# Two attentions in one kernel: x^T of the second batch loaded a stage sooner, first scores in turns with queries, turned P written ahead of x, x in whole rows at the start

## The chip, the cores and the metric

The kernel runs on one core of one Trainium2 chip. A core has engines that run beside each other, each with its own list of instructions in a fixed order: PE (TensorE, the matrix products), DVE (VectorE), ACT (ScalarE), POOL (GpSimd) and SP (SyncE, which here issues nearly all DMAs). An instruction waits by semaphore for what it needs, and everything behind it on its engine waits too. The metric is the device time of a run in microseconds. Three runs of the kernel before took 825.4, 826.2 and 827.56 us; their median is 826.2 us.

## The reference

x is (2, 2048, 640), two batches of 2048 rows; the context is (2, 128, 384), of which the last 4 tokens are the adapter's. There are 8 heads of 80 columns; all is float32.

```python
enc, ca = ctx[:, :124], ctx[:, 124:]
query = x @ Wq
hs = mha(query, enc @ Wk, enc @ Wv)              # text attention, 124 keys
ca_q1 = einsum('btc,th->bch', ca, Wq_ca)          # (2, 384, 640)
ca_q1 = ca_q1[:, linspace(0, 383, 2048).astype(int), :]
ca_hs1 = mha(ca_q1, x, x)                         # keys and values are x itself
ca_hs2 = mha(ca_hs1 @ Wq, ca @ Wk_ca, ca @ Wv_ca) # 4 keys
out = (hs + ca_hs2) @ Wout + b_out + x
```

mha is softmax(q k^T / sqrt(80)) v by heads. The second attention has only 384 different query rows in a batch, so the kernel computes those and gathers its rows by index at the end.

## The kernel before, in words

**Blocks.** x is worked on in 8 blocks of 512 rows, (b, sb) with b the batch and sb from 0 to 3, and in 16 row tiles of 128 a batch. Products with Wq need x transposed. Block (0, 0) is loaded plainly into a buffer "xz" and transposed on PE (pt_x, `x_first`). Every other block comes by `x_block`: 8 DMAs (xi) gather pieces of 128 bytes into the same buffer "xz", of which there is one, and five DVE transposes of 32x32 squares (xt) finish the job. The transposed blocks lie in five slots (`Slots`); a block's slot is given back when its users are done. `slots.free(n)` is a condition on them. In the second batch each block is loaded twice: once for yz, once more ("again") for its queries.

**Adapter attention** for a batch: `yz_block` (pyz, pt_y) maps a block to its logits' factors, `maxima` makes scores s and reduces their maxima on DVE (mx), `less_maxima` folds the maxima in, and `contraction` makes the scores again, takes exp on ACT (ea) and accumulates against y (acc). Scores s go through one PSUM buffer of four banks, so an s waits for the engine that reads the one before.

**Text attention**: `queries` makes q of a block (pq, 5 column chunks c, each summed over 5 row chunks i of x^T), `scores` takes a unit m of two row tiles (sc, then maximum m and subtraction on DVE, exp on ACT, sum r on DVE, product on POOL), `turned` transposes P on DVE (eb), writes it to HBM (kept) and reads it back by keys (pT), `values` multiplies with the values and Wout (ph, po) and adds into the residual rows xo, which `residual` has loaded. `completed` adds gathered rows of the adapter to tiles that were stored early (xe, early).

**Order.** PE's instructions and SP's DMAs stay in the order in which the program writes them. That order is made by a small planner: a `Fill` is a list of stages that yield after pieces of PE work, `Mix` runs the fill that has had the least PE time (by its own costs), and `weave` runs a main line (the setup, maxima, contraction) and fills each gap, given in us, with pieces. `own` holds adapter blocks, `text` the queries and units, `again` the second loads. `together` steps several generators in turns, `chain` one after the other. `ahead(m)` is what is done for unit m: the residual and the turned P of unit m + 1, scores of unit m + 2, queries, and the values of m. A scheduler orders the other engines' instructions by their readiness. Pools set how much can be open: PSUM tiles of `mm_tile` come three at a time from ps_m, "xrow" holds four row tiles x, P turned (eb) and pT have one buffer each.

**The lines that the steps touch.** L345 to 365 load x, Wq and the first weights; L633 `x_first`; L647 `x_block`; L836 `queries`; L896 `turned`, L912 `residual`, L1034 `ahead`; from L1061 the plan.

Of the kernel before, what the change touches and what calls it, by code (L numbers as in the profile page):

```python
# [13 lines left out]
P = 128  # L14
# [135 lines left out]
def kernel(  # L150
# [194 lines left out]
    def load_grouped(dst, w):  # L345
        dma(dst[:, :4, :], w.rearrange("(c r) n -> r c n", c=4)[:P])
        for g in range(4):
            dma(dst[R * g : R * (g + 1), 4, :], w[D2 * g + P : D2 * (g + 1), :])

# [7 lines left out]
    for st in range(4):  # L357
        most, rest = by_chunk(x[0, st * P : (st + 1) * P, :])
        t = rows_of[:, st]
        dma(t[:, : 4 * P].rearrange("p (c d) -> p c d", c=4), most)  # L360
        dma(t[:, 4 * P :].rearrange("p (g d) -> p g d", g=4), rest)
        if st == 2:
            load_grouped(wq_sb, Wq)
# [269 lines left out]
    def x_first():  # L633

        t = x_tile(0, 0, False)
        flat = t.rearrange("p k c s -> p (k c s)")
        for n in range(4 * NCH):
            k, c = divmod(n, NCH)
            if n % 4 == 0:
                pt = mm_tile(f"pt_x_{n // 4}")  # L640
            transpose(
                pt[:, n % 4 * P : (n % 4 + 1) * P], rows_of[:, k, c * P : (c + 1) * P], ident
            )
            if n % 4 == 3:
                evacuate(flat[:, (n - 3) * P : (n + 1) * P], pt)
# [190 lines left out]
    def queries(n, chunks):  # L836

        t = xt["q", *blocks[n]]
        if n not in q_of:
            yield from room(n)  # L840
        for c in chunks:
# [192 lines left out]
    def ahead(m):  # L1034
# [4 lines left out]
        if m + 1 < units:  # L1039
            more = [residual(m + 1), turned(m + 1)]  # L1040
# [38 lines left out]
    Mix(pe, (text, 1)).run(5.0)  # L1079
# [3 lines left out]
    for sb in range(NSB):  # L1083
# [5 lines left out]
    text.add(  # L1089
        stage(("s", 0), scores(0)), stage("turned", together(turned(0), residual(0))),  # L1090
        stage(("s", 1), scores(1)),
        *[ahead(m) for m in range(units)],
    )
    weave(less_maxima(0, mx_of[0]), fill)
    ps_turns[:] = [ps_m]
    on[0] = "D"
    own.add(adapter_stages("x", 1, 0, slots.free(1), ("q", *blocks[NSB - 1])))
# [6 lines left out]
    own.add(adapter_stages("yz", 1, 0))  # L1104
    for sb in range(1, NSB):
        own.add(
            adapter_stages("x", 1, sb, slots.free(1)),
            adapter_stages("yz", 1, sb, ("half", 1, sb - 1)),
        )
# [3 lines left out]
            stage(("again", 1, sb), x_block(1, sb, True), slots.free(2), ("t", 2 * sb + 2))  # L1113
# [48 lines left out]
```

## Time and profile before

| | before |
|---|---|
| median of 3 runs | 826.2 us (825.4 to 827.56) |
| the profiled execution | 825.36 us, span 823.7 us |
| PE busy | 754.6 us (92%) |
| DVE, ACT, POOL busy | 379.4 (46%), 191.1 (23%), 134.5 (16%) us |
| mean granted TensorE clock | 0.969 |
| chain that ended last | PE 78%, DVE 8%, DMA 6%, SPq 2%, issue 2%, ACT 2%, POOL 1% |
| DMA moved | 96.94 MB in 151029 packets, 120197 of them under 512 B |

The span runs from the first to the last instruction of the profiled execution; its device time is 1.66 us longer. PE is the engine that is busy nearly all the time, and the chain of work that ended last goes through it for 78% of the span. The mean granted clock is a share of the full 2.4 GHz; in single stretches it is 1.0 or falls to 0.5. "SPq" and "PEq" are the sequencers of an engine, which issue DMAs or wait. The matmul's own line is L28, a helper's, so rows are told apart by the names of their tiles.

### The profile page before, as it was taken

Reading aid. Unit: us, or ns where it says so; the run is one execution under the profiler, and the core shown is the slowest. Engines: PE = TensorE matmul, PEld = TensorE weight load, DVE = VectorE, ACT = ScalarE, POOL = GpSimd, SP = SyncE. Lnnn points to the kernel's source line nnn. Section 1 sums busy time; section 2 is a strip of 40 time slices with the busy share of each in tenths; the row PEclk is TensorE's granted clock in tenths of the full one; section 3 lists DMA queues with packets and bytes.
Section 4 is the critical chain, followed back from the end, with each engine's and each line's share of the span. In section 5 each row is a group of like instructions: output and inputs, shape, how many; then the busy total and the mean of one; then the engine's idle time right before and its main releaser. Section 6 shows DMA issues by size and latency. Waiting matters only on the chain.

```text
span 823.7 us, 9364 instructions
## 1 busy us (share of the span) xinstructions
PE 754.6 (92%) x3785; PEld 386.3 (47%) x3785; DVE 379.4 (46%) x507; ACT 191.1 (23%) x232; POOL 134.5 (16%) x192
## 2 busy tenths in 40 slices
PE   4999999999779999981999997999999999999987
PEld 3663343333434445550444453543443456556654
DVE  1124655442743426563574956452230375255621
ACT  2021221113434344100212020044443421011100
POOL 6000000000111003220050503010010012542320
PEclk9999999999979999995999998999999999999999
DMA  9708414000152415676797984081320545977771
GB/s 250 171 1 134 63 13 64 1 0 1 52 167 68 128 40 153 192 133 96 186 207 165 214 204 84 21 187 38 99 52 17 85 146 156 249 203 191 211 205 63
DMA packets 151029, 96.94 MB, mean 118 GB/s; under 512 B 120197, under 2 KB 122565, under 8 KB 148938
## 3 DMA queue, kind: packets, MB, share of 16 engines
q1 hardware_dynamic: 145866, 85.75, 41.1%
q0 software_dynamic: 5120, 10.59, 8.0%
q8 instruction: 30, 0.49, 0.3%
q14 instruction: 13, 0.11, 0.0%
HBM read 64.14 MB, written 32.18 MB: 117 GB/s over the span
## 4 chain that ended last, share of the span: by engine, by line
PE 78%; DVE 8%; DMA 6%; SPq 2%; issue 2%; ACT 2%; POOL 1%; DVEq 0%; ACTq 0%; POOLq 0%
PE pq L28 21%; PE po L28 19%; PE s L28 11%; PE sc L28 8%; PE acc L28 5%; PE ph L28 5%; PE pyz L28 3%; SPq L222 2%; DMA pT<-kept 2%; DMA kept<-eb 2%; DVE xt L660 2%; DVE mx L711 2%; POOL p L892 1%; DVE p L880 1%; DMA xz<-in_x_dram 1%
## 5 line engine op out<-in xcount | busy, mean ns | idle before, releaser
L28 PE MATMUL po<-wout_sb,hsT 128*128 128x320 f32 x640 | 187.0, 440 | 0.0
L28 PE MATMUL pq<-xt,wq_sb 128*128 128x512 f32 x320 | 155.0, 621 | 7.0 <-DVE xt L660 5.8
L28 PEld LDWEIGHTS po<-wout_sb,hsT 128*128 128x128 f32 x640 | 119.7, 191 | 68.9 <-issue 24.8
L711 DVE TENSOR_REDUCE mx<-s 128x4 f32<-128x2048 f32 x48 | 109.5, 2281 | 84.8 <-PE s L28 84.8
L892 POOL TENSOR_TENSOR p<-p,r 128x992 f32<-128x992 f32 x32 | 61.3, 1915 | 438.5 <-DVE r L891 378.9
L761 ACT ACTIVATE ea<-s 128x1536 f32<-128x1536 f32 x64 | 92.6, 1447 | 107.0 <-PE s L28 107.0
L28 PEld LDWEIGHTS pq<-xt,wq_sb 128*128 128x128 f32 x320 | 59.6, 197 | 84.7 <-issue 72.4
L28 PE MATMUL sc<-kpad,q 128*128 128x248 f32 x384 | 96.8, 390 | 1.6 <-DVE r L775 1.6
L961 DVE TENSOR_TENSOR xo<-xo,po 128x320 f32<-128x320 f32 x64 | 30.4, 479 | 121.2 <-PE po L28 121.2
L28 PEld LDWEIGHTS sc<-kpad,q 128*128 128x128 f32 x384 | 69.7, 192 | 34.6 <-issue 22.1
L28 PE MATMUL s<-ca,yz 32*128 32x384 f32 x512 | 60.9, 545 | 6.2 <-ACT ea L761 6.0
L879 DVE TENSOR_REDUCE m<-sc 128x4 f32<-128x496 f32 x64 | 42.5, 664 | 42.7 <-PE sc L28 42.5
L28 PE MATMUL ph<-pT,vpad 128*32 128x256 f32 (+1 forms) x512 | 53.6, 399 | 9.0 <-DMA pT<-kept 8.6
L28 PE MATMUL s<-yz,ca 32*128 32x512 f32 x384 | 54.8, 640 | 5.7 <-DVE mx L711 5.5
L243 ACT COPY q<-pq 128x512 f32<-128x512 f32 x31 | 18.1, 585 | 172.1 <-PE pq L28 172.1
L901 DVE STREAM_TRANSPOSE eb<-p 128x1024 f32<-128x1024 f32 x32 | 39.1, 1234 | 40.8 <-POOL p L892 37.2
L28 PE MATMUL acc<-ea,y_sb 128*32 128x384 f32 x512 | 55.9, 509 | 0.0
L887 ACT ACTIVATE p<-p 128x992 f32<-128x992 f32 x32 | 33.0, 1030 | 96.4 <-DVE p L880 96.4
L973 POOL DMA_INDIRECT xo<-o,query x23 | 36.0, 1565 | 78.0 <-DVE m L879 29.9
L890 DVE TENSOR_REDUCE r<-p 128x8 f32<-128x992 f32 x32 | 37.8, 1181 | 19.4 <-ACT p L887 19.4
L880 DVE TENSOR_TENSOR p<-sc,m 128x496 f32<-128x496 f32 x64 | 42.9, 670 | 1.8
L28 PE MATMUL pyz<-xt,wyz 128*64 128x512 f32 (+1 forms) x96 | 25.3, 648 | 19.5 <-DVE xt L660 19.5
(137 smaller groups left out, 433.8 us busy)
## 6 DMA issues: line engine op xcount, KB each, us to landing
kept<-eb SPq DMA_DIRECT2D x16, 1024.0 KB, 5.7
pT<-kept SPq DMA_DIRECT2D x64, 256.0 KB, 5.4
xi<-in_x_dram SPq DMA_DIRECT2D x44, 256.0 KB, 4.8
xo<-in_x_dram SPq DMA_DIRECT2D x32, 320.0 KB, 3.5
out_dram<-xo SPq DMA_DIRECT2D x23, 320.0 KB, 2.3
early<-xo SPq DMA_DIRECT2D x9, 320.0 KB, 2.4
xe<-early SPq DMA_DIRECT2D x9, 320.0 KB, 7.0
out_dram<-xe SPq DMA_DIRECT2D x9, 320.0 KB, 3.2
```

The lines of the kernel that those rows point to most:

```text
L28: ins = self.tc.nc.tensor.matmul(out, lhsT, rhs, **kw)
L243: nc.scalar.copy(dst, src)
L711: nc.vector.tensor_reduce(mx[:, ct, u, :, sb], q4, AX.X, ALU.max)
L761: nc.scalar.activation(e, q4[:, :, :CAD], AF.Exp, scale=SCALE)
L879: nc.vector.tensor_reduce(m, s4, AX.X, ALU.max)
L880: nc.vector.tensor_tensor(e[:, 4 * u : 4 * u + 4, :NK], s4, m.unsqueeze(2).to_broadcast([P, 4, NK]), ALU.subtract,)
L887: nc.scalar.activation(et, et, AF.Exp, scale=SCALE)
L890: nc.vector.tensor_reduce(r, et, AX.X, ALU.add)
L892: nc.gpsimd.tensor_tensor(et, et, r.unsqueeze(2).to_broadcast([P, HEADS, NK]), ALU.mult)
L901: nc.vector.transpose(eb[:, :, k], e_of.pop(at).rearrange("p h (j b) -> p j h b", j=4))
L961: nc.vector.tensor_tensor(xr[k][:, cols], xr[k][:, cols], po[:, :HALF], ALU.add)
L973: nc.gpsimd.indirect_dma_start(out=t, out_offset=None, in_=o2_of[b], in_offset=bass.IndirectOffsetOnAxis(ap=query[:, st : st + 1], axis=0) ...
```

## The change

**Start.** The first block of x is loaded in four DMAs of whole rows (128x640) ahead of Wq, and four DVE copies collect each tile's last columns into x_last; before, each tile came in two DMAs, the last tile behind Wq. Wq comes in four DMAs of one chunk each and four small ones; before, the four chunks were one DMA. The first three column chunks of block 0's queries are now summed in turns over the row chunks i, in three PSUM tiles, and the share of text work ahead of the setup is 12.5 us of planned PE time instead of 5.0.

**First scores.** The scores of units 0 and 1 and the turned P of unit 0 run in turns with the query stages that are left, where they stood behind all of them.

**Turned P ahead of x.** In `ahead`, the turned P of the next unit (eb, kept) is written before its residual rows xo are loaded.

**Second batch.** Blocks 0 and 1 of the second batch are both loaded during the first contraction (block 1 was loaded at the start of the second maxima). The "again" loads for the queries may start with one free slot instead of two, and one unit sooner.

```diff
--- before.py
+++ after.py
@@ -342,11 +342,6 @@
 
     load_ca(0)
 
-    def load_grouped(dst, w):
-        dma(dst[:, :4, :], w.rearrange("(c r) n -> r c n", c=4)[:P])
-        for g in range(4):
-            dma(dst[R * g : R * (g + 1), 4, :], w[D2 * g + P : D2 * (g + 1), :])
-
     w_c = {}
 
     def load_w(name, w):
@@ -354,13 +349,12 @@
         dma(w_c[name], w.rearrange("(c p) n -> p c n", p=P))
 
     rows_of = block_rows("xz").rearrange("p (k n) -> p k n", k=4)
-    for st in range(4):
-        most, rest = by_chunk(x[0, st * P : (st + 1) * P, :])
-        t = rows_of[:, st]
-        dma(t[:, : 4 * P].rearrange("p (c d) -> p c d", c=4), most)
-        dma(t[:, 4 * P :].rearrange("p (g d) -> p g d", g=4), rest)
-        if st == 2:
-            load_grouped(wq_sb, Wq)
+    for k in range(4):
+        dma(rows_of[:, k], x[0, k * P : (k + 1) * P, :])
+    for c in range(4):
+        dma(wq_sb[:, c, :], Wq[D2 * c : D2 * c + P, :])
+    for g in range(4):
+        dma(wq_sb[R * g : R * (g + 1), 4, :], Wq[D2 * g + P : D2 * (g + 1), :])
     load_w("kca", Wk_ca)
     load_w("k", Wk)
 
@@ -634,13 +628,18 @@
 
         t = x_tile(0, 0, False)
         flat = t.rearrange("p k c s -> p (k c s)")
+        last = xrow.tile([P, H], F32, tag="x", name="x_last")[:, : 4 * P]
+        last = last.rearrange("p (k s) -> p k s", k=4)
+        for k in range(4):
+            nc.vector.tensor_copy(
+                last[:, k, :].rearrange("p (g d) -> p g d", g=4), by_chunk(rows_of[:, k, :])[1]
+            )
         for n in range(4 * NCH):
             k, c = divmod(n, NCH)
             if n % 4 == 0:
                 pt = mm_tile(f"pt_x_{n // 4}")
-            transpose(
-                pt[:, n % 4 * P : (n % 4 + 1) * P], rows_of[:, k, c * P : (c + 1) * P], ident
-            )
+            src = rows_of[:, k, D2 * c : D2 * c + P] if c < 4 else last[:, k, :]
+            transpose(pt[:, n % 4 * P : (n % 4 + 1) * P], src, ident)
             if n % 4 == 3:
                 evacuate(flat[:, (n - 3) * P : (n + 1) * P], pt)
 
@@ -838,6 +837,19 @@
         t = xt["q", *blocks[n]]
         if n not in q_of:
             yield from room(n)
+        if n == 0:
+
+            first, chunks = chunks[:3], chunks[3:]
+            pq = [mm_tile(f"pq_{n}_{c}") for c in first]
+            for i in range(NCH):
+                for c in first:
+                    matmul(
+                        pq[c], wq_of(i, c), t[:, :, i, :], start=(i == 0), stop=(i == NCH - 1)
+                    )
+                yield WITHIN
+            for c in first:
+                evacuate(q_of[n][:, c, :], pq[c])
+            yield
         for c in chunks:
             pq = mm_tile(f"pq_{n}_{c}")
             for i in range(NCH):
@@ -1037,7 +1049,7 @@
 
         parts, needs, more = [], [], []
         if m + 1 < units:
-            more = [residual(m + 1), turned(m + 1)]
+            more = [turned(m + 1), residual(m + 1)]
         more.append(completed())
         if m + 2 < units:
             parts.append(stage(("s", m + 2), scores(m + 2)))
@@ -1076,7 +1088,7 @@
         adapter_stages("yz", 0, 3, ("half", 0, 2)),
     )
     text = Fill(done, *[early(n) for n in range(NSB)])
-    Mix(pe, (text, 1)).run(5.0)
+    Mix(pe, (text, 1)).run(12.5)
     fill = Mix(pe, (own, 1), (text, 1))
     weave(setup_a2(), fill)
     own.parts.insert(0, adapter_stages("yz", 0, 0))
@@ -1086,23 +1098,22 @@
     fill.until(done, "values")
     sp_stack.close()
     open_late()
-    text.add(
-        stage(("s", 0), scores(0)), stage("turned", together(turned(0), residual(0))),
-        stage(("s", 1), scores(1)),
-        *[ahead(m) for m in range(units)],
+    first = chain(
+        stage(("s", 0), scores(0)), together(turned(0), residual(0)), stage(("s", 1), scores(1))
     )
+    text.parts[:] = [together(first, *text.parts), *[ahead(m) for m in range(units)]]
     weave(less_maxima(0, mx_of[0]), fill)
     ps_turns[:] = [ps_m]
     on[0] = "D"
-    own.add(adapter_stages("x", 1, 0, slots.free(1), ("q", *blocks[NSB - 1])))
+    own.add(adapter_stages("x", 1, 0, slots.free(1)), adapter_stages("x", 1, 1, slots.free(1)))
     weave(contraction(0, sq, 2.0), fill)
 
 
     begin(1)
     on[0] = "A"
     ps_turns[:] = [ps_m, ps_m, ps_m, ps_a]
-    own.add(adapter_stages("yz", 1, 0))
-    for sb in range(1, NSB):
+    own.add(adapter_stages("yz", 1, 0), adapter_stages("yz", 1, 1, ("half", 1, 0)))
+    for sb in range(2, NSB):
         own.add(
             adapter_stages("x", 1, sb, slots.free(1)),
             adapter_stages("yz", 1, sb, ("half", 1, sb - 1)),
@@ -1110,7 +1121,7 @@
     again = Fill(
         done,
         *[
-            stage(("again", 1, sb), x_block(1, sb, True), slots.free(2), ("t", 2 * sb + 2))
+            stage(("again", 1, sb), x_block(1, sb, True), slots.free(1), ("t", 2 * sb + 1))
             for sb in range(NSB)
         ],
     )
```

The order of the setup on PE: the last key product pk, the pa products of the adapter's key, and the first queries of block 1 (pq from xt_1; xt_0 is block 0). Before:

```order
32 L28 MATMUL pk_372<-ctxT,k_279 128x256 x3
33 L41 MATMUL pt_wq_0_381<-ident,wq_sb 128x128 x4
34 L41 MATMUL pt_wq_4_387<-ident,wq_104 128x128
35 L28 MATMUL pq_3_429<-xt_0_196,wq_sb 128x512
36 L28 MATMUL pa_301<-blk_kca,wqT_380 128x48 x5
37 L28 MATMUL pq_3_429<-xt_0_196,wq_sb 128x512 x2
38 L41 MATMUL pt_wq_0_439<-ident,wq_sb 128x128 x4
39 L41 MATMUL pt_wq_4_445<-ident,wq_104 128x128
40 L28 MATMUL pq_3_429<-xt_0_196,wq_sb 128x512 x2
41 L28 MATMUL pa_301<-blk_kca,wqT_438 128x48 x5
42 L28 MATMUL pq_4_456<-xt_0_196,wq_104 128x512 x5
43 L28 MATMUL pyz_0_0_472<-xt_0_196,wyz 64x512 x2
```

Here the queries of block 0 (pq_3, pq_4) stand between the last pk and pyz. After the change, with the same names:

```order
54 L28 MATMUL pk_400<-ctxT,k_292 128x256 x3
55 L28 MATMUL pa_317<-blk_kca,wqT_390 128x48 x5
56 L28 MATMUL pq_0_453<-xt_1_275,wq_sb 128x512 x2
57 L41 MATMUL pt_wq_0_457<-ident,wq_sb 128x128 x4
58 L41 MATMUL pt_wq_4_463<-ident,wq_104 128x128
59 L28 MATMUL pq_0_453<-xt_1_275,wq_sb 128x512 x2
60 L28 MATMUL pa_317<-blk_kca,wqT_456 128x48 x5
61 L28 MATMUL pq_0_453<-xt_1_275,wq_sb 128x512
62 L28 MATMUL pyz_0_0_484<-xt_0_195,wyz 64x512 x2
```

The first query product of block 1 moved to a place directly behind the last pk and one group of pa, and the pyz of block 0 now has one query product in front of it instead of five.

DVE, in the same place of the program after the change (kpad is made from pk, wyz from pa, xt_1 is the transposed block 1 for that query):

```order
26 L508 TENSOR_SCALAR kpad<-pk_357,side 128x2x124 x2
27 L508 TENSOR_SCALAR kpad<-pk_400,quarter 128x2x124 x4
28 L659 STREAM_TRANSPOSE xt_1_275<-xi_1_276 128x512 x4
29 L662 STREAM_TRANSPOSE xt_1_275<-xi_1_276 128x4x128
30 L399 TENSOR_SCALAR wyz<-pa_317,side 128x4x24
31 L402 TENSOR_SCALAR wyz_107<-pa_317,halves 128x24
32 L399 TENSOR_SCALAR wyz<-pa_317,side 128x4x24
33 L402 TENSOR_SCALAR wyz_107<-pa_317,halves 128x24
```

The transposes of block 1 moved from behind the wyz operations to the place between kpad and wyz.

The second maxima, SP's list. Before, xi_0, xi_1 and xi_2 are the loads for yz of the second batch, and kept, pT, xo belong to text units:

```order
87 L222 DMA xi_0_1917<-in_x_dram 32x16x32
88 L222 DMA pT_1952<-kept_1833 32x4x512 x4
89 L222 DMA xi_1_1971<-in_x_dram 32x64x32
90 L222 DMA xi_1_1971<-in_x_dram 32x16x32
91 L222 DMA xi_1_1971<-in_x_dram 32x64x32
92 L222 DMA xi_1_1971<-in_x_dram 32x16x32
93 L222 DMA xi_1_1971<-in_x_dram 32x64x32
94 L222 DMA xi_1_1971<-in_x_dram 32x16x32
95 L222 DMA xi_1_1971<-in_x_dram 32x64x32
96 L222 DMA xi_1_1971<-in_x_dram 32x16x32
97 L222 DMA out_dram<-xo_6_1631 128x640
98 L222 DMA xi_2_2063<-in_x_dram 32x64x32
```

The loads of blocks 1 and 2 for yz stand one behind the other, with one store between. After the change, xi_0 and xi_1 here are the second loads for queries, and xi_2 is block 2 for yz, some rows later in the list:

```order
99 L222 DMA xi_1_2032<-in_x_dram 32x16x32
100 L222 DMA kept_2049<-eb_2046 128x2048
101 L222 DMA xo_10_2051<-in_x_dram 128x640
102 L222 DMA xo_11_2053<-in_x_dram 128x640
103 L222 DMA xe_0_2055<-early_0_1366 128x640
104 L222 DMA xe_0_2055<-early_1_1414 128x640
105 L222 DMA xe_2_2058<-early_2_1577 128x640
106 L222 DMA xe_2_2058<-early_3_1626 128x640
107 L222 DMA xi_2_2126<-in_x_dram 32x64x32
108 L222 DMA xi_2_2126<-in_x_dram 32x16x32
```

The load of block 1 for yz has moved forward into the first contraction, and the second loads of blocks 0 and 1 have taken the places ahead of block 2.

DVE around those loads, after the change (mx are maxima of the adapter's scores, xo_9 a residual tile, eb the turned P, xt the transposed blocks):

```order
229 L973 TENSOR_TENSOR xo_8_1835<-xo_8_1835,po_8_1_2216 128x320
230 L710 TENSOR_REDUCE mx_1924<-s_1_1_0_1_2225 128x4
231 L710 TENSOR_REDUCE mx_1924<-s_1_1_1_0_2242 128x4
232 L973 TENSOR_TENSOR xo_9_1837<-xo_9_1837,po_9_0_2238 128x320
233 L659 STREAM_TRANSPOSE xt_1_2031<-xi_1_2032 128x512 x4
234 L662 STREAM_TRANSPOSE xt_1_2031<-xi_1_2032 128x4x128
235 L710 TENSOR_REDUCE mx_1924<-s_1_1_1_1_2260 128x4
236 L913 STREAM_TRANSPOSE eb_2321<-p_12_2062 128x4x256
237 L913 STREAM_TRANSPOSE eb_2321<-p_13_2153 128x4x256
238 L659 STREAM_TRANSPOSE xt_2_2125<-xi_2_2126 128x512 x4
239 L662 STREAM_TRANSPOSE xt_2_2125<-xi_2_2126 128x4x128
240 L710 TENSOR_REDUCE mx_1924<-s_1_1_2_0_2291 128x4
```

The transposes that empty the buffer of xi_1 stand behind xo_9_0, and those of xi_2 behind one mx and two eb. PE beside it:

```order
385 L28 MATMUL po_9_0_2238<-wout_sb,hsT_0_2075 128x320 x2
386 L28 MATMUL po_9_0_2238<-wout_sb,hsT_2_2145 128x320
387 L28 MATMUL s_1_1_1_0_2242<-yz_1_2096,ca_129 128x512 x4
388 L28 MATMUL po_9_0_2238<-wout_sb,hsT_2_2145 128x320
389 L28 MATMUL po_9_0_2238<-wout_sb,hsT_4_2170 128x320
390 L28 MATMUL pq_2_2255<-xt_0_1972,wq_sb 128x512 x4
391 L28 MATMUL s_1_1_1_1_2260<-yz_1_2096,ca_129 128x512 x4
392 L28 MATMUL pq_2_2255<-xt_0_1972,wq_sb 128x512
393 L28 MATMUL pyz_2_0_2269<-xt_2_2125,wyz 64x512 x2
394 L28 MATMUL pyz_2_1_2270<-xt_2_2125,wyz 64x512 x2
395 L28 MATMUL pyz_2_0_2269<-xt_2_2125,wyz_107 128x512
396 L28 MATMUL pyz_2_1_2270<-xt_2_2125,wyz_107 128x512
```

pyz of block 2 stands one query chunk and one s behind the last po_9_0.

The last unit, SP's list, before:

```order
214 L222 DMA out_dram<-xo_10_3814 128x640
215 L222 DMA out_dram<-xo_11_3816 128x640
216 L222 DMA xo_14_4040<-in_x_dram 128x640
217 L222 DMA xo_15_4042<-in_x_dram 128x640
218 L222 DMA kept_4047<-eb_4044 128x2048
219 L222 DMA pT_4076<-kept_4047 32x4x512 x4
```

The store of kept stands behind two stores and two loads. After the change:

```order
207 L222 DMA out_dram<-xo_10_3823 128x640
208 L222 DMA out_dram<-xo_11_3825 128x640
209 L222 DMA kept_4047<-eb_4044 128x2048
210 L222 DMA xo_14_4049<-in_x_dram 128x640
211 L222 DMA xo_15_4051<-in_x_dram 128x640
212 L222 DMA pT_4080<-kept_4047 32x4x512 x4
```

The store of kept moved ahead of the two loads of xo.

## Rows read from the trace of the kernel before

**Rows 1.** Page, totals: the span, and PE's busy time, share and instructions.
```profile
span 823.7 us, 9364 instructions
PE 754.6 (92%) x3785; PEld 386.3 (47%) x3785; DVE 379.4 (46%) x507; ACT 191.1 (23%) x232; POOL 134.5 (16%) x192
```

**Rows 2.** Waits of PE: us in total, times, longest.
```profile
PE pyz L28 <- DVE xt L660: 19.5, 1, 19.5
PE ph L28 <- DMA pT<-kept: 8.6, 2, 4.4
PE pt_x L41 <- DMA xz<-in_x_dram: 7.9, 2, 7.7
PE s L28 <- ACT ea L761: 6.0, 3, 4.4
PE pq L28 <- DVE xt L660: 5.8, 1, 5.8
PE s L28 <- DVE mx L711: 5.5, 3, 2.9
```

**Rows 3.** Stretch by PE, PEld, DVE, ACT, POOL busy; granted clock, DMA share, GB/s.
```profile
380.00:390.00 10.00, 0.00 (x0) 0.00 (x0) 0.19 (x1) 0.00 (x0) 0.00 (x0) 0.50 1.01 158
```

**Rows 4.** Timeline, start: start us, us long, engine, operation, [idle before <- releaser].
```profile
5.86 3.66 SPq L222 DMA_DIRECT2D wq_sb<-in_L_xattn_Wq_dram  x5
...
19.08 7.40 PE L28 MATMUL pq<-xt,wq_sb 128*128 128x512 f32 x12
26.32 0.84 PE L28 MATMUL p_kca<-caT,w_kca 128*128 128x8 f32 x7
```

**Rows 5.** Timeline of PE, 176 to 211, at the full clock.
```profile
176.58 5.42 PE L28 MATMUL pq<-xt,wq_sb 128*128 128x512 f32 x12
...
206.49 0.93 PE L28 MATMUL s<-ca,yz 32*128 32x384 f32 x8
207.35 0.85 PE L28 MATMUL acc<-ea,y_sb 128*32 128x384 f32 x8
208.13 2.78 PE L28 MATMUL sc<-kpad,q 128*128 128x248 f32 x12
```

**Rows 6.** DMA issues, 4 to 20: KB each, median us to landing.
```profile
wq_sb<-in_L_xattn_Wq_dram SPq DMA_DIRECT2D x1, 1280.0 KB, 10.0
...
xz<-in_x_dram SPq DMA_DIRECT2D x3, 64.0 KB, 8.0
```

**Rows 7.** Timeline, setup: PE's pa, DVE's kpad.
```profile
38.32 1.21 PE L28 MATMUL pa<-blk_kca,wqT 128*128 128x48 f32 x10
...
51.92 1.63 DVE L514 TENSOR_SCALAR kpad<-pk,quarter 128x248 f32<-128x248 f32 x4 [0.44 <-PE pk L28]
```

**Rows 8.** Timeline, first unit: ACT's exp, SP's store of kept, PE's first ph.
```profile
216.16 1.03 ACT L887 ACTIVATE p<-p 128x992 f32<-128x992 f32 x1 [2.71 <-DVE p L880]
...
222.54 0.36 SPq L222 DMA_DIRECT2D kept<-eb  x1
...
236.10 1.98 PE L28 MATMUL ph<-pT,vpad 128*64 128x256 f32 x8 [4.36 <-DMA pT<-kept]
```

**Rows 9.** Timeline, second batch: transposes, the next load, the pyz behind it.
```profile
375.13 2.48 DVE L660 STREAM_TRANSPOSE xt<-xi 128x512 f32<-128x512 f32 x4
...
378.23 9.10 SPq L222 DMA_DIRECT2D xi<-in_x_dram  x8
...
392.36 1.97 PE L28 MATMUL pyz<-xt,wyz 128*64 128x512 f32 x4 [19.50 <-DVE xt L660]
```

**Rows 10.** Timeline of SP: an x load while POOL issues gathers.
```profile
423.24 16.64 SPq L222 DMA_DIRECT2D xi<-in_x_dram  x8
```

**Rows 11.** Timeline, the last unit: SP's xo loads and kept, PE's last first ph.
```profile
787.30 2.20 SPq L222 DMA_DIRECT2D xo<-in_x_dram  x2
...
789.55 0.42 SPq L222 DMA_DIRECT2D kept<-eb  x1
...
804.39 4.58 PE L28 MATMUL ph<-pT,vpad 128*64 128x256 f32 x32 [4.25 <-DMA pT<-kept]
```

## The prediction

> **What bounds the kernel now.** I read the page's totals first: TensorE (PE) is busy 754.6 us, 92% of the span [rows 1]. Of what is left, almost all stands in one view, the waits of PE by what it waited for [rows 2]: 19.5 us once for the transposes of x (xt) ahead of pyz, 8.6 in two waits for the turned P (pT), 7.9 at the start for x, 6.0 for an exp, 5.8 for another xt, 5.5 for maxima. So a change gains only by shortening those waits, or by keeping the granted clock up: while PE stood still before the second batch, 0.50 was granted [rows 3], the 1.2 GHz level, and work behind a long wait starts at that level. Twelve pq matmuls took 7.40 us right after the first wait [rows 4] and 5.42 elsewhere [rows 5], so that dip cost 2.0; I price every dip behind a wait of over 4 us like it. The work of PE itself is the same before and after, so I go by stalls alone, place by place, against the profiled run of 825.36 us (span 823.7 and 1.66 around it); the median of the runs shown, 826.2, lies 0.84 above it.
>
> **1. Start: x in whole rows, Wq by chunks, three query chunks in turn.** In before the fourth tile of x is issued behind Wq, and PE waits for it; the queries start at 19.08 and p_kca, which needs its own weights, at 26.32 [rows 4]. In after all of x is issued ahead of Wq. The first Wq load went out at 5.86 [rows 4], where after's first will, and the load of 1280 KB needed 10.0 us to land [rows 6]. I take x complete at about 9, the last transposes and copies until about 12, and then queries paced by PE, with Wq's chunks landing one by one until 16 or 17: 15 chunk products (30 matmuls) at 5.42/12 x 2 = 0.9 us are 13.5, with 2.0 for the clock this gives 27.5 for p_kca. That is 1.2 later than before, but 9 products more are done, 9 x 0.9 = 8.1. Gain 6.9, I take 7. Bounds: 8.5 if p_kca comes at 26, 0 if x and Wq still land only at 18 together.
> Here the trace shows one Wq issue of 1280 KB that landed in 10.0 us with other loads in flight [rows 6]; no row of it shows Wq in smaller pieces. The Trainium skill ("DMA: Bandwidth & Descriptors", section "Measured (HBM→SBUF, 128 partitions, SWDGE, issued from GpSimd)") asks for loads batched to 1 MiB and more and calls transfers under 64 KB dominated by descriptors; by it the four pieces of 320 KB are a step back, and the sum would be that of rival (c) below.
>
> **2. The setup behind it: a new stall.** Because the queries of block 0 are done sooner, PE reaches the first query of block 1 before the vector engine (DVE) has its x^T. On DVE four kpad operations, 1.63 us [rows 7], and four transposes of x, 2.48 [rows 9], stand between the last pk and that query, 4.1 us in a row; PE has only pa in between, 1.21 [rows 7]. Stall 4.1 - 1.2 = 2.9, plus 0.9 for a clock dip (less than half of 2.0, since the stop is short). Then pyz of block 0 waits for wyz: eight small DVE operations, which I take for as long as the four of kpad and a little more, 1.8, with one query product (0.9) in front, where before five covered them: 0.9. Together +4.7, between +1 (if pk comes earlier against pa) and +7.
>
> **3. First contraction: the first scores.** The second score tile ends at 208.13 + 2.78 = 210.9 [rows 5]; its exp starts at 216.16, kept is issued at 222.54, ph comes at 236.10 [rows 8]: 25.2 us in all. Meanwhile PE had five score banks of 1.4 (half of 2.78) and four pairs of s and acc of 1.64 (206.49 to 208.13 [rows 5]), 13.5, so it lost 11.7 there. Of the 5.3 until the exp, most is DVE's work for the first tile (its sum, its eb). In after the first tile's scores come some 20 us before the second's, so only the second's own maximum and subtraction are left: between 0 and 5.3, I take 2.3, nearer to nothing. From exp to ph it stays 19.9 (236.10 - 216.16): 22.2. But one pair of s and acc fewer lies in it: cover 11.9, loss 10.3. Net -1.4, and the dips as before. Block 1's x load, 8 more DMAs on SP right behind pT (9.10 us of issue [rows 9]), shares the queues with pT: bounds -5 and +4.
>
> **4. Second batch: x^T a stage sooner.** Before: the 19.5, and behind it 2.9 and 0.9 of the waits for maxima and 5.8 for the xt of the queries [rows 2], 29.1, with three dips of 2.0: 35.1. The buffer "xz" holds one x load at a time: in before DVE's transposes start at 375.13, the next load is issued at 378.23 (3.1 later), and PE goes on at 392.36 [rows 9]: 14.1 from issue to PE. In after block 1 is there early, so these waits go. But the order shows the two query blocks (xi_0 and xi_1 again) going through that one buffer ahead of block 2, and DVE empties xi_1 only behind xo_9_0. From the end of po_9_0 on PE I take 1.7 for what DVE still does (the rest of a maxima reduction, and xo), then the transposes 3.1: xi_2 is issued 4.8 after it. PE has pq_2 (5 x 0.9 = 4.5) and one s (about 1.1), 5.6. So pyz_2 waits 4.8 + load - 5.6: a smaller form of the removed wait. The load is the unknown: 14.1 if the queues are as free as in [rows 9]; where gathers ran on POOL, the same eight issues took 16.64 us [rows 10] instead of 9.10, so 21.6. In after the gathers of four early tiles (xe) end about when xi_2 is issued, so I take the middle, 17.9: wait 17.1. With a dip of 2.0 and 1.0 for later maxima, 20.1. Net -15.0; bounds -19 and -9.
>
> **5. Second contraction and end.** In the second contraction the exp waits change little: +0.4 for one s more in a row. At the end kept is issued ahead of the two xo loads: it went at 789.55, behind xo's issues from 787.30, of which the second sat until the output store had landed; pT followed, and ph waited 4.25 until 804.39 [rows 11]. In after kept goes at about 787.3, 2.2 sooner, and without 640 KB ahead of it in the queues, worth about 1.2 more: -3.4, and part of the dip, -0.8: -4.2. The xo loads come some 0.4 later, under 11 us of po. The same swap in the middle units costs nothing: nobody waits for pT there. Bounds -6 and 0.
>
> **Sum.** -7.0 + 4.7 - 1.4 - 15.0 + 0.4 - 4.2 = -22.5. Profiled run 802.9, median 803.7.
>
> **Rivals.** (a) The wait only moves: the xi_2 load meets all the gathers, 21.6, and DVE is late with xi_1 by 2: pyz_2 waits 5.7 more than I take, 809.4. For it: the load with gathers beside it was that slow [rows 10]. Against: the four gathers are issued some ten us sooner by my count. (b) The scores in turns hide the first unit fully: the 6.0 for the exp shrinks by its 4.4, ph's first 4.3 goes and two dips of 2.0, so 12.7 instead of 1.4, giving 792.4. Against: in the order the second score tile still stands only five banks ahead of ph. (c) Small pieces land later: 64 KB pieces of x took 8.0 us in before [rows 6]; if the chunks of Wq come no sooner than before, PE waits for them in turn, and the start gains nothing: 810.7. (d) Slower: two loads in series in front of pyz_2. SP stores xo_7, which waits for its gather, ahead of xi_1's issues; if that store hangs until after po_9_0, xi_1 is loaded only then, and pyz_2 waits one load and its transposes more, 17.9 + 3.1 + 1.0 = 22.0 at the middle price and 25.7 at 21.6: 826 to 829. It decides from a gather that ends 15 us or more after po_7: by the order PE has about 36 us of work between po_7 and po_9_0, and a load of 21.6 fits behind any sooner gather. (e) That the change does nothing is excluded by the order, in which block 1 and the pieces are moved.
>
> **How the numbers follow.** Forecast 0.54, (a) 0.20, (c) 0.12, (b) 0.08, (d) 0.04, and 0.02 for small losses that add up to the whole gain. The range 792 to 816 holds the forecast with its bounds, where they don't all fall the same way, (a), (b), (c), and (a) with (c) (816.4) nearly. A change of 0.3%, 2.5 us, is what a measurement here tells from none. Slower needs (d) with the slow load or losses elsewhere: 0.03. Same, (d) at its middle price and the added losses: 0.04. Faster 0.93.
>
> **What would show it.** Right: no wait of PE at pyz of block 1; a wait of 13 to 21 us at pyz of block 2 for xt, and the clock at half behind it; the pq wait of 5.8 gone; the first query at about 12 and p_kca near 27; a stall of 3 at the first query of block 1; the first unit's ph wait still there, with the exp's 6 us or more; the last ph wait under 1. Wrong: Wq's last chunk landing after 18; pyz_2 waiting over 25 or under 8; pT of the first unit landed before PE asks for it.

## The result and the profile after

The changed kernel takes 804.61 us (median of 4 runs, 801.64 to 809.19) against 826.88 for the kernel before (825.4 to 827.56) on the same chip: a ratio of 0.9738, interval 0.9684 to 0.9792. In a second series, e11 below, it took 806.11, ratio 0.9761 [0.9733, 0.9788]. The profiled execution took 802.71 with a span of 801.0; that of before took 825.36 with 823.7 [rows 1]. So 22.65 us went between the two profiled runs, and the forecast was 22.5.

The page's totals after:

```profile
span 801.0 us, 9355 instructions
PE 750.4 (94%) x3785; PEld 384.3 (48%) x3785; DVE 381.1 (48%) x511; ACT 191.6 (24%) x232; POOL 134.4 (17%) x192
```

Against [rows 1], PE runs the same 3785 instructions; its busy time is 4.2 us shorter, because less of it ran at the low clock (mean granted clock 0.979 against 0.969). The other 18 us of the gain must be waits. The waits of PE after (what was waited for; us in total, times, longest) answer to [rows 2]:

```profile
PE pyz L28 <- DVE xt L659: 15.0, 1, 15.0
PE s L28 <- ACT ea L760: 6.4, 6, 2.8
...
PE ph L28 <- DMA pT<-kept: 3.5, 1, 3.5
PE po L28 <- DVE o L245: 3.2, 1, 3.2
PE pq L28 <- DVE xt L659: 3.2, 1, 3.2
PE s L28 <- DVE mx L710: 2.9, 3, 1.8
PE pt_x L41 <- DVE wqcaT L391: 2.3, 1, 2.3
```

The 19.5 for xt at pyz has become one of 15.0, and it is another wait: for block 2, no longer for block 1. The 7.9 for x at the start, one of the two waits for pT and the 5.8 of the queries are gone. Three of over 2 us are new: 3.2 for a copy (o), 3.2 for transposes of the setup, 2.3 at the start for wqcaT. The timeline after shows each place (start us, us long, engine, operation, in brackets the idle time before and what ended it):

```profile
13.03 13.14 PE L28 MATMUL pq<-xt,wq_sb 128*128 128x512 f32 x30
...
26.01 2.74 PE L28 MATMUL p_kca<-caT,w_kca 128*128 128x8 f32 x24
...
31.19 3.04 PE L28 MATMUL pq<-xt,wq_sb 128*128 128x512 f32 x4
...
52.99 1.63 DVE L508 TENSOR_SCALAR kpad<-pk,quarter 128x248 f32<-128x248 f32 x4 [8.45 <-PE pk L28]
54.53 2.48 DVE L659 STREAM_TRANSPOSE xt<-xi 128x512 f32<-128x512 f32 x4
...
57.15 3.52 PE L28 MATMUL pq<-xt,wq_sb 128*128 128x512 f32 x4 [3.16 <-DVE xt L659]
...
64.99 3.00 PE L28 MATMUL pyz<-xt,wyz 128*64 128x512 f32 x12
...
205.67 2.78 PE L28 MATMUL sc<-kpad,q 128*128 128x248 f32 x12
...
209.02 1.03 ACT L899 ACTIVATE p<-p 128x992 f32<-128x992 f32 x1 [2.49 <-DVE p L892]
...
215.01 0.35 SPq L222 DMA_DIRECT2D kept<-eb  x1
...
228.07 1.98 PE L28 MATMUL ph<-pT,vpad 128*64 128x256 f32 x8 [3.53 <-DMA pT<-kept]
...
341.09 1.25 DVE L913 STREAM_TRANSPOSE eb<-p 128x1024 f32<-128x1024 f32 x1 [0.85 <-POOL p L904]
342.26 0.85 DVE L245 COPY o<-po 128x320 f32<-128x320 f32 x2
...
342.77 1.34 PE L28 MATMUL po<-w_sb,p2T 65*128 65x320 f32 x4 [3.24 <-DVE o L245]
...
345.88 3.80 PE L28 MATMUL pyz<-xt,wyz 128*64 128x512 f32 x12
...
403.70 1.34 PE L28 MATMUL po<-wout_sb,hsT 128*128 128x320 f32 x4
...
409.54 10.18 SPq L222 DMA_DIRECT2D xi<-in_x_dram  x8
...
413.81 1.54 POOL L985 DMA_INDIRECT xe<-o,query  x1 [0.56 <-issue]
...
423.04 2.49 DVE L659 STREAM_TRANSPOSE xt<-xi 128x512 f32<-128x512 f32 x4 [8.86 <-DMA xi<-in_x_dram]
...
425.59 4.85 PE L28 MATMUL pyz<-xt,wyz 128*64 128x512 f32 x12 [14.99 <-DVE xt L659]
...
770.48 0.42 SPq L222 DMA_DIRECT2D kept<-eb  x1
...
771.00 1.65 SPq L222 DMA_DIRECT2D xo<-in_x_dram  x2
...
783.29 2.95 PE L28 MATMUL ph<-pT,vpad 128*64 128x256 f32 x32
```

Read it from the top. The queries start 6 us sooner than in [rows 4] and run 30 in a row at full speed (13.14/30 = 0.44 each); the low clock comes later, four pq in 3.04. In the setup the transposes sit behind kpad, and PE waits 3.16 for them. The exp starts 2.0 after the second score tile (the first half of the sc row, until 207.06), where it was 5.3 in [rows 8]. At 342.77 PE waits for the copy o, which stands on DVE behind eb, and eb waits for POOL; this wait was not in before. In the second batch xi is issued 4.5 after the end of po (405.04), PE goes on 16.05 after the issue (three gathers of xe run beside the load, the first at 413.81), and the twelve pyz behind the wait take 4.85 where twelve at 64.99 took 3.00. The clock agrees: 0.53 was granted there, the 1.2 GHz level, against 0.50 in [rows 3] (stretch by PE, PEld, DVE, ACT, POOL busy; granted clock, DMA share, GB/s):

```profile
420.00:430.00 10.00, 4.41 (x12) 1.18 (x12) 3.08 (x5) 0.00 (x0) 0.00 (x0) 0.53 1.15 247
```

At the end kept goes out ahead of xo, and the last ph starts without a wait, against 4.25 in [rows 11].

### The profile page after: what moved, and what is told of

Its sections match the earlier page's. It is cut to its first block, busy times and chain, and to the rows that moved or that the text cites. A ratio compares the mean times of both kernels' runs of the same rounds, so it can differ in the third digit from the quotient of the medians.

```text
span 801.0 us, 9355 instructions
## 1 busy us (share of the span) xinstructions
PE 750.4 (94%) x3785; PEld 384.3 (48%) x3785; DVE 381.1 (48%) x511; ACT 191.6 (24%) x232; POOL 134.4 (17%) x192
## 4 chain that ended last, share of the span: by engine, by line
PE 83%; DVE 7%; DMA 4%; ACT 2%; issue 2%; SPq 1%; POOL 1%; DVEq 0%; ACTq 0%; POOLq 0%
PE po L28 22%; PE pq L28 21%; PE s L28 12%; PE sc L28 8%; PE ph L28 5%; PE acc L28 5%; PE pyz L28 3%; DVE xt L659 1%; DVE mx L710 1%; DMA kept<-eb 1%; SPq L222 1%; PE pt_y L41 1%; DVE m L891 1%; PE pk L28 1%; DVE p L892 1%
## 5 line engine op out<-in xcount | busy, mean ns | idle before, releaser
L28 PE MATMUL pq<-xt,wq_sb 128*128 128x512 f32 x320 | 152.9, 614 | 3.7 <-DVE xt L659 3.2
```

Source lines behind the costliest of these rows:

```text
L28: ins = self.tc.nc.tensor.matmul(out, lhsT, rhs, **kw)
```

## The experiments

Every ratio is to the kernel before, timed beside the run, and stands with its interval; the changed kernel is at 0.9738 and 0.9761. The first four take back one part of the change each.

**e1: the start undone.**

```diff
-    for k in range(4):
-        dma(rows_of[:, k], x[0, k * P : (k + 1) * P, :])
...
+        if st == 2:
+            load_grouped(wq_sb, Wq)
...
-        if n == 0:
...
-    Mix(pe, (text, 1)).run(12.5)
+    Mix(pe, (text, 1)).run(5.0)
```

> The start alone as before (x tiles in two pieces with the last behind Wq, Wq in one load of four chunks, no turns, 5.0 us of queries ahead of the setup), the other three parts as in the changed kernel. Theory: the start gains more than the setup behind it gives back. By the prediction undoing it costs 7.0 - 4.7 = 2.3 us; by the two traces PE's loss up to the first pyz was 4.0 us smaller after the change, so I now expect 808.5 against 804.6, with the wait for x of 7.7 back and the 3.2 wait for xt of block 1 gone. Rival: the pieces of Wq cost what the order gains; then undoing it changes nothing (804 to 805).

Measured: 802.51, 0.9718 [0.969, 0.9745], no slower than the changed kernel. The 6.8 us for x are back, but the planner now makes another order: the load of block 2 goes ahead of xi_1 "again", and the wait at pyz_2 is gone altogether (last row: no idle time before pyz). In its place one x load stands on SP between kept and pT, and PE waits 13.4 for pT. Timeline of e1:

```profile
222.37 0.36 SPq L222 DMA_DIRECT2D kept<-eb  x1
222.97 10.78 SPq L222 DMA_DIRECT2D xi<-in_x_dram  x8
...
235.21 1.76 SPq L222 DMA_DIRECT2D pT<-kept  x4
...
243.94 1.97 PE L28 MATMUL ph<-pT,vpad 128*64 128x256 f32 x8 [13.44 <-DMA pT<-kept]
...
419.93 3.00 PE L28 MATMUL pyz<-xt,wyz 128*64 128x512 f32 x12
```

So the parts don't add up: taking one back moves the others' instructions. What the loads at the start are worth needs a kernel that keeps PE's order, which is e5.

**e2: the first scores undone.**

```diff
-    first = chain(
-        stage(("s", 0), scores(0)), together(turned(0), residual(0)), stage(("s", 1), scores(1))
+    text.add(
+        stage(("s", 0), scores(0)), stage("turned", together(turned(0), residual(0))),
+        stage(("s", 1), scores(1)),
+        *[ahead(m) for m in range(units)],
```

> The first scores again behind all queries instead of in turns with them, the rest as in the changed kernel. Theory (prediction): the chain from the second score tile to ph is 1.4 us shorter with the turns; the traces say 25.2 us before and 21.1 after, with one pair of s and acc fewer beside it, so some 2.5 to 3.5 us net: 807 to 808. Rival: the 3.2 us wait for the copy of o and the low clock behind it (5.5 us together), which only the changed kernel shows at 339 us, come from the units running earlier; then undoing the turns takes them away too and the time is 801 to 803.

Measured: 811.13, 0.9831 [0.9809, 0.9853], so the turns are worth 6 to 8 us (0.9831 less 0.9761 or 0.9738). At the place itself a wait must be read with the clock behind it. Timeline of PE in e2:

```profile
217.05 1.90 PE L28 MATMUL sc<-kpad,q 128*128 128x248 f32 x6 [2.04 <-DVE p L892]
219.42 1.66 PE L28 MATMUL s<-ca,yz 32*128 32x384 f32 x8 [0.47 <-ACT ea L760]
...
228.79 1.98 PE L28 MATMUL ph<-pT,vpad 128*64 128x256 f32 x8 [6.27 <-DMA pT<-kept]
```

Idle time is 8.8 here, and the instructions around take 4.7 more than at the full clock (s 1.66 for 0.93, ph 1.98 for 1.08, and so on): 13.5 lost. Counted alike, before lost 13.7 (4.4 + 4.4 and 5.0), after 10.7 (2.8 + 3.5 and 4.4), and e11, where ph waited 6.1 but PE had the full clock ahead of it, 10.5. So 3 of the 6 to 8 us stand here; PE is 4.5 later at pyz of block 1 (376.78 against 372.24) and 7.9 at pyz of block 3 (472.61 against 464.69), and what lies between isn't placed. The wait for o stays at 3.2, now at a ph, so the turns of the scores did not cause it.

**e3: xo ahead of the turned P again.**

```diff
-            more = [turned(m + 1), residual(m + 1)]
+            more = [residual(m + 1), turned(m + 1)]
```

> The residual loads again ahead of the turned P, the rest as in the changed kernel. Theory: at the end kept again goes 2 us later, behind an xo load that waits for a store, and the last ph waits 4 us with a dip of about 2: 809 to 811 (the prediction priced this part at 4.2). Rival: the end is paced by something else and the wait was only an effect of the units' phase; then 804 to 806.

Measured: 810.61, 0.9821 [0.9791, 0.9851]. The last wait for pT is back. Timeline of e3:

```profile
771.75 2.20 SPq L222 DMA_DIRECT2D xo<-in_x_dram  x2
...
774.00 0.42 SPq L222 DMA_DIRECT2D kept<-eb  x1
...
789.07 4.63 PE L28 MATMUL ph<-pT,vpad 128*64 128x256 f32 x32 [4.47 <-DMA pT<-kept]
```

kept goes out 2.25 behind xo, as in [rows 11], and the 32 ph behind the wait take 4.63 instead of 2.95: the dip alone is 1.7. 

**e4: the second batch undone.**

```diff
-    own.add(adapter_stages("x", 1, 0, slots.free(1)), adapter_stages("x", 1, 1, slots.free(1)))
+    own.add(adapter_stages("x", 1, 0, slots.free(1), ("q", *blocks[NSB - 1])))
...
-    for sb in range(2, NSB):
+    for sb in range(1, NSB):
...
-            stage(("again", 1, sb), x_block(1, sb, True), slots.free(1), ("t", 2 * sb + 1))
+            stage(("again", 1, sb), x_block(1, sb, True), slots.free(2), ("t", 2 * sb + 2))
```

> Block 1 of the second batch loaded at the start of its maxima again, the query loads with two free slots, as before; the rest as in the changed kernel. Theory: the stall of 19.5 us at pyz of block 1, its smaller companions and the xt wait of 5.8 at the queries come back, the 15.0 us at pyz of block 2 goes: +15 by the prediction, +17.5 by the traces: 819 to 822. Rival: the waits before hung on the phase of the text units, which the other parts have shifted; then part of it stays away and the time is under 814.

Measured: 819.22, 0.9931 [0.991, 0.9952]: 14 to 16 us are this part's. PE waits at pyz of block 1 as in [rows 9], and its queries wait for xt again, 9.7 in two waits. Timeline of e4:

```profile
394.75 4.77 PE L28 MATMUL pyz<-xt,wyz 128*64 128x512 f32 x12 [22.46 <-DVE xt L659]
```

**e5: only the loads of x and Wq undone; the order of PE stays that of the changed kernel.**

```diff
-    for c in range(4):
-        dma(wq_sb[:, c, :], Wq[D2 * c : D2 * c + P, :])
...
+        if st == 2:
+            load_grouped(wq_sb, Wq)
...
-            src = rows_of[:, k, D2 * c : D2 * c + P] if c < 4 else last[:, k, :]
```

> Only the loads at the start as before (x tiles in two pieces, the last behind Wq, Wq's four chunks in one load); the turns of the queries and every later instruction keep the changed kernel's order. So this shows the loads without the planner's answer to them. Theory: the last tile of x lands at about 17 to 18 again, the queries start at 18 to 19 instead of 13.0, and 5 to 7 us are lost and stay lost: 809 to 812 against 804.6. Rival (rule on small pieces): pieces of 320 KB are slower than one load, so the loads of before cost nothing more: 804 to 806. The run before that undid the whole start measured no loss (802.5), but in it the planner set the later order differently (no 15 us wait at pyz of block 2, 13.4 at the first ph).

Measured: 811.96, 0.9834 [0.9792, 0.9875]; its runs spread from 807.87 to 819.62. PE waits 8.2 for x, the same 30 pq start at 19.20, and p_kca comes at 34.40 instead of 26.01. At this place the loads are worth 8.4 us, of which 6 to 8 reach the end; its interval only just clears that of e11. Rival (c), by which they gain nothing, falls.

**e10 and e11: Wq's four chunks in one load, and the changed kernel once more.**

```diff
-    for c in range(4):
-        dma(wq_sb[:, c, :], Wq[D2 * c : D2 * c + P, :])
+    dma(wq_sb[:, :4, :], Wq.rearrange("(c r) n -> r c n", c=4)[:P])
```

> Wq's four chunks in one load of 1280 KB behind x, the four small pieces as they are; all else as in the changed kernel. By the rule on small pieces the one load is faster as a whole and lands before the last of four; by my theory the first query needs only the first chunk, which landed at 10.25, and PE begins at 13.0 anyway because x is transposed until then; the one load lands at 13 to 15. Theory: queries begin up to 2 us later, 805 to 807. By the rule: no later than now, 803 to 804.6.

> The changed kernel unaltered, beside the two above on one chip, for a narrower interval: 802 to 806.

Measured: e10 809.5, 0.9802 [0.9778, 0.9826]; e11 806.11, 0.9761 [0.9733, 0.9788]. One load is about 3.4 us slower, though the intervals just touch. It landed 9.5 us after its issue, at 13.04; the queries started at 13.17, behind a stop of 0.62, and ran slowly at first. Timeline of e10, whose profiled run is the slowest of its six:

```profile
12.59 0.59 ACT L243 COPY xt<-pt_x 128x512 f32<-128x512 f32 x1 [0.27 <-PE pt_x L41]
...
13.17 15.52 PE L28 MATMUL pq<-xt,wq_sb 128*128 128x512 f32 x30 [0.62 <-ACT xt L243]
```

The view puts the stop down to ACT. But this copy ended at 13.18, behind the start, and the one before it at 12.33; what came last ahead of 13.17 was Wq, at 13.04. So the landing cost 0.6 directly. The first six products took 5.22, twice their usual time, and the thirty 2.4 more than after; PE came to the first pyz at 68.85, 3.4 later than in e11. That the stop cost this rate isn't shown: the thirty took 14.09 in e3 and 13.88 in e12, which start as after does and without such a stop, against 13.14 after. e11 shows something else: the same program as after, with a wait of 19.3 at pyz_2 instead of 15.0 and one of 6.1 at the first ph (counted in e2). Timeline of e11:

```profile
409.79 10.90 SPq L222 DMA_DIRECT2D xi<-in_x_dram  x8
...
414.06 1.54 POOL L985 DMA_INDIRECT xe<-o,query  x1 [0.56 <-issue]
...
430.13 4.44 PE L28 MATMUL pyz<-xt,wyz 128*64 128x512 f32 x12 [19.28 <-DVE xt L659]
```

The load was issued at the same time as after, but took 20.3 to PE instead of 16.05: its first piece landed in 4.3 us, the seventh in 11.2, where these took 4.2 and 7.1 after. The gathers of xe alone don't make the difference, for the same three run beside the load in both, from 413.81 after and from 414.06 here. This wait makes up the 4.1 us between the two profiled executions; the other executions have no trace.

**e6: block 2 loaded ahead of the second query block.**

```diff
-            stage(("again", 1, sb), x_block(1, sb, True), slots.free(1), ("t", 2 * sb + 1))
+            stage(("again", 1, sb), x_block(1, sb, True), slots.free(1), ("t", 2 * sb + 1), *([("x", 1, sb + 1)] if 0 < sb < NSB - 1 else []))
```

> One condition more: the second load of block 1 (for the queries) waits until block 2's load for yz is issued, and that of block 2 until block 3's. The order then has xi_2 directly behind the first units' stores and xi_1 again behind it. Theory: the 15.0 us wait at pyz of block 2 is the one buffer, filled with xi_1 which isn't needed for another 50 us; it goes, with its low clock (2 to 3 us), and nothing takes its place: 786 to 789. Rival: the loads are slow because of gathers and stores on the queues wherever they stand; then a wait of 8 us or more comes back at pyz of block 2 or 3 or at the queries of block 1: 795 to 800.

Measured: 799.63, 0.9678 [0.9658, 0.9697]. Timeline of e6:

```profile
415.07 5.48 PE L28 MATMUL pyz<-xt,wyz 128*64 128x512 f32 x12 [3.76 <-DVE xt L659]
...
432.53 1.97 PE L28 MATMUL ph<-pT,vpad 128*64 128x256 f32 x8 [4.76 <-DMA pT<-kept]
```

The wait of 15.0 shrinks to 3.8, so the order of the two loads through the one buffer did cause it. Only 5 to 7 us of the 11 reach the end: pT now stands behind the x load on SP (8 issues from 415.63, pT at 424.41), ph waits 4.8, and the clock dips at both places.

**e7 and e8: two of DVE's jobs on ACT, which has room.** e7 moves the last four kpad, e8 the copy o.

```diff
-                nc.vector.tensor_scalar(kpad[:, :, 2 * c + i, :], pk3, of, None, ALU.mult)
+                if c < 4:
+                    nc.vector.tensor_scalar(kpad[:, :, 2 * c + i, :], pk3, of, None, ALU.mult)
+                else:
+                    nc.scalar.activation(kpad[:, :, 2 * c + i, :], pk3, AF.Copy, scale=of)
```

> The four last kpad products are made on ACT instead of DVE, nothing else. Theory: the 3.2 us wait at the first query of block 1 is DVE's order: the transposes of block 1 stand behind these four, although their data landed at 32 and DVE was idle from 44.5 to 53.0. In the order of this kernel they stand directly behind the fourth chunk's kpad, so they run at about 45, and the wait and the low clock behind it (1.6) go: 799.5 to 801. Rival: only the 1.6 us of the four products go, or ACT's copies of wqT come late and PE waits for those: 803 to 805.

```diff
-                evacuate(o2[:, cols], po[:, :HALF])
+                nc.scalar.copy(o2[:, cols], po[:, :HALF])
```

> The copies of o (the adapter's output rows) at the end of a contraction are made on ACT instead of DVE or in turns. Theory: the 3.2 us wait of PE at 339 us for such a copy comes from DVE's order, in which the copy stands behind the eb transpose, which waits for POOL; on ACT it comes at once, and the low clock behind (2.5) goes too: 798.5 to 800.5. Rival: PE then waits at the same place for ph's or sc's PSUM copies on DVE instead: 803 to 805.

Measured: e7 800.82, 0.9696 [0.9677, 0.9714]. DVE's transposes of block 1 start 10 us sooner and PE never waits for them. Timeline of e7:

```profile
43.88 2.48 DVE L662 STREAM_TRANSPOSE xt<-xi 128x512 f32<-128x512 f32 x4
...
52.47 1.54 ACT L511 ACTIVATE kpad<-pk,quarter 128x248 f32<-128x248 f32 x4 [1.05 <-PE pk L28]
53.26 1.95 PE L28 MATMUL pq<-xt,wq_sb 128*128 128x512 f32 x4
```

e8: 803.73, 0.9736 [0.9702, 0.9769]. The wait for o falls from 3.2 to 0.5, and 1.7 of it comes back at ph, for p. The interval holds the changed kernel's ratios, so the trace shows the wait go, but the time does not tell a gain from none.

**e9: all three edits, with a later condition on the query block, `("t", 2 * sb + 2)` beside `("x", 1, sb + 1)`.**

> Together: block 2's load ahead of the query load of block 1 and pT ahead of that load too (its condition is one unit later), the last kpad products on ACT, the copies of o on ACT; all else as in the changed kernel. In the run with block 2 first, PE lost 3.8 at pyz of block 2 (a maxima reduction ahead of its transposes on DVE) and 4.8 at the next ph, because both x loads' 16 DMAs stood on SP ahead of that unit's pT. Theory: putting xi_1 behind pT takes the 4.8 and its dip (1.5) away; with 5.0 from block 2 first, 3.8 from kpad, 1 to 3 from o: 788 to 791. Rival: the text unit's chain has no slack there and the wait only moves to the next pT or to the queries of block 1: 794 to 797.

Measured: 804.61, 0.9743 [0.9716, 0.977], no gain over the changed kernel. The pyz wait is 3.8, but the later query blocks bring two other waits, 8.7 at ph (xi issued from 448.33 stands ahead of kept at 458.31) and 7.6 at s for a maximum.

**e12: the condition of e6 with both edits of e7 and e8.** It adds nothing to the diffs of those three.

> Block 2's load ahead of the query load of block 1 as in the run that did this alone (the query load keeps its early place, directly behind it), with the last kpad products and the copies of o on ACT. In the combined run before, the query load stood later, just ahead of the next unit's kept and pT, and two new waits came (8.7 at that unit's ph, 7.6 for a maximum behind the late transposes). Theory: the place of that load is what lost 15 us there; with the early place the three edits add up to about 5.0 + 4.0 + 1 to 3 from the changed kernel's 804.6 to 806.1: 793 to 796. Rival: the edits on ACT shift the units and cost what they give: 799 to 801.

Measured: **793.21** (791.03 to 798.77), 0.963 [0.9601, 0.966], faster than before and than the changed kernel. The waits of PE in e12:

```profile
PE ph L28 <- DMA pT<-kept: 10.8, 2, 5.9
...
PE pyz L28 <- DVE xt L662: 3.8, 1, 3.8
...
PE ph L28 <- DVE p L895: 1.7, 1, 1.7
```

What is left is mostly pT: 5.9 behind an x load on SP (8 issues from 406.59, pT at 415.56), and 4.9 in the first unit, where pT went out at 214.36, ahead of the x load of 216.16. A second buffer for x rows, so that no load waits for another, wasn't tried.

## Why the prediction was right

The time was right within 1 us and the mechanism was right in its parts; that the sum came out closer than its terms is luck, because their errors cancelled. By the prediction's steps, in profiled runs:

| Step | forecast | measured | from |
|---|---|---|---|
| 1 and 2, start and setup | -2.3 | -3.9 | first pyz 64.99 (64.61 before), 5 query products of 0.86 more done |
| 3, first contraction | -1.4 | -1.3 | -3.0 at the first unit, 13.7 before and 10.7 after (e2); other waits of the contraction 1.2 before and 2.9 after |
| 4, second batch | -15.0 | -17.5 | before 29.1 of waits and 5.5 of low clock behind them; after 15.0, a dip of 1.85 and 0.2 of maxima |
| 5, second contraction | +0.4 | -0.7 | PE's waits from 520 us on, other than for pT, 2.9 before and 2.2 after |
| 5, end | -4.2 | -5.9 | wait 4.25, and 32 ph in 2.95 for 4.58 |
| not foreseen | 0 | +4.9 | the wait for o, 3.2, and the low clock behind it, 1.6 |
| not foreseen | 0 | +1.6 | maxima of the first batch, 1.8 before and 2.6 after; yz at pt_y, 3.1 before and 3.9 after |

These terms add up to -22.8, against -22.65 measured.

**Step 1** took the first query for 12 and p_kca for 27.5; they came at 13.03 and 26.01. The first Wq load went out at 3.59 and not at 5.86, as taken, and still the start was later: four new copies of x_last, each waiting for its x tile (the last landed at 9.08), stand on DVE ahead of wqcaT, and PE waited 2.3 for it. The 2.0 for the clock did not come there: the 30 products ran at full speed. The Trainium skill ("DMA: Bandwidth & Descriptors", section "Measured (HBM→SBUF, 128 partitions, SWDGE, issued from GpSimd)") asks for loads of 1 MiB and more. As a price of time this did not hold here, where SP issues the loads: three of the 320 KB pieces landed 6.7 to 7.7 us after issue (of the fourth the profile tells no landing), the single 1280 KB load 9.5, and the kernel with the single load was slower, by 0.6 for its landing and 2.4 for the rate of its first products in the profiled run (e10).

**Step 2** forecast a stall of 2.9, and 3.16 was measured; the dip behind it was 1.6 (four pq in 3.52 for 1.88), where 0.9 was forecast, and the wait at wyz (0.9) did not come. e7 shows its cause: without the kpad ahead of the transposes it goes.

**Step 3** put the exp 2.3 behind the second score tile and the chain to ph at 22.2; measured 2.0 and 21.0. The net of -1.4 came out, but as -3.0 at this place and +1.7 by other waits of the contraction, for exps above all, which the step left out. By e2 the whole part is worth 6 to 8 us, of which its trace places 3 here; the rest lies in later stretches and is open.

**Step 4**, the largest term, was right as a mechanism: the wait moved to block 2, behind two query blocks in one buffer. The step's numbers were xi_2 issued 4.8 after po_9_0, a load of 17.9, a wait of 17.1; measured 4.5, 16.05 and 15.0, and in e11 20.3 and 19.3. The middle value taken for the load stood in the middle of these two runs, but its reason did not hold: the four gathers were to end about when xi_2 is issued, and three of them ran beside the load, the first from 413.81. So the size was partly luck. The mechanism is shown by e4 (the part undone) and e6 (the order turned).

**Step 5** had the wait and the swap right (e3) and the dip too small, 0.8 for 1.6.

**The miss** is the wait for o at 342.77. The prediction went from wait to wait of the kernel before, and this one was not among them at such a size: it lies where the new order puts a copy for PE behind an operation that waits for POOL. e8 takes it away. Of the runs that take back a part, e2 to e5 keep it at 3.2, and only e1 is without it. As e5 undoes the loads of the start alone, this points to the rest of the start, the turns of the queries and the larger share ahead of the setup, by the order that the planner makes of them; one run in another order does not prove it.

**The rivals.** (a), the slow load with gathers, in part: the load did meet three of the four gathers, but took 16.05 and 20.3 us instead of 21.6, and in e11 the wait came to 19.3 of the 22.8 that it gave. (b), the first unit hidden fully, no: 3.5 stay at ph. (c) no: e5. (d), two loads in series, no: xi_1 was transposed at 406.44, right behind po_9_0, as forecast.

## What to carry to other kernels

Removing a wait for a load moves it to the next user of the same buffer; look for that user in the order first, and price it by the same load's slowest and fastest rows. Look at what stands ahead of a needed instruction on an engine or queue that is itself idle: here a copy behind an operation waiting for POOL, four kpad ahead of transposes, and an x load between a store and its read-back each cost PE 3 to 13 us. Where a planner makes the order, undoing a part is no measure of it unless the order stays; hold the order fixed (e5) before giving a part a price.

## What the runs showed of the hardware

- The eight issues of one x load hold SP's queue for 8.7 to 11 us at most places shown here, and longer at others, 14.86 at the start of the changed kernel or 16.64 in [rows 10], so that everything behind them on SP waits as long.
- One program's load took 16.05 us to PE in one execution and 20.3 in another, with the same issue times; the pieces issued in its first 3 us landed in 4.1 to 4.6 us, the seventh in 7.1 in the one and in 11.2 in the other, with the same three gathers beside it. What made the difference is open.
- At the very start the column of the granted clock did not tell the rate: in e10 it read 1.00 from 12 to 28, yet the first six pq took 0.87 each, the time of the low clock, and later ones 0.44. The trace's first record of the clock begins at 18.03 there, and at 13.03, with the first pq, in the changed kernel; ahead of the first record the column reads 1.00 with nothing recorded. There the durations are to be read.
